# A two-layer graph network on one core: transposes a step ahead, node stages in three places of a step

## The chip, the cores and the metric

The kernel runs on one core of a Trainium2 chip. The metric is the device time in microseconds of one launch; the number given for a kernel is the median of several launches. Besides, one launch is recorded by the hardware profiler, and everything said of single instructions comes from that recorded launch.

## The reference

A graph of N = 6250 nodes with 256 features, and E = 106250 directed edges (50000 in both directions and a loop at each node), sorted by destination. All is fp32. With x the nodes and `e` the edge features, the reference computes, for layer 0,

```
msg = relu(x[src] + e);            agg = segment_sum(msg, dst)
h   = x + x + agg;                 f   = gelu(bn1(h) @ W1.T + b1) @ W2.T + b2
x1  = layernorm(x + bn2(h + f))
```

and for layer 1, on x1,

```
m    = gelu((x1[src] + e) @ W1m + b1m) @ W2m + b2m
mean = segment_sum(m, dst) / max(degree, 1)
u    = gelu(mean @ W1u + b1u) @ W2u + b2u
out  = layernorm(x1 + layernorm(x1 + u) * gamma + beta)
```

## The kernel before, in words

**Tiles, windows, blocks.** The edges are cut into 831 tiles of 128, and eight tiles make a window (SPAN), in two groups of four: 104 windows. Nodes are taken in 25 blocks of 256 (24 full ones and a rest of 106). Because edges are sorted by destination, the edges of a window end in a short run of nodes, in one block or in two neighbours; a block is complete after some 4.2 windows.

**What a window goes through.** `gather` (L768, L772) fetches the source rows of its eight tiles, with one indirect DMA per tile on GpSimd's queue (POOL), into one of five ring buffers. `lifted` (L804) copies a pair of edge tiles into a PSUM bank on ScalarE (ACT), and `add_to_gathered` (L812) adds that on VectorE (DVE) to the gathered rows in place. `activated` (L820) applies ReLU or GELU to a group of four tiles on ACT. `one_hots` (L828) makes eight 128x32 one-hot matrices on DVE. `into_slots` (L847) multiplies them with the eight tiles on TensorE (PE), which sums the edges of each of up to 128 slots, and ACT copies the sums out of PSUM. `into_blocks` (L863) multiplies the sums with a second one-hot matrix and so adds them to the block's accumulator, in layer 0 also the degrees (L886 on PE, L890 on DVE). In layer 0, `opened_0` (L1000) starts an accumulator with eight products of the block's own rows (L1006).

**Products with W1m.** Both layers need products of edge rows with W1m. Layer 1 takes x1 @ W1m + b1m, which the node stages of layer 0 have stored as `proj`, gathers its rows by source, and adds e @ W1m. `turned` (L779) transposes a pair of edge tiles on PE (four transposes, L785) into the one bank of `eaP`, and ACT copies them to SBUF (`eaT`, L790, three buffers). `product` (L793) multiplies them with W1m on PE (L798). Layer 0 computes those products for the first group of each window and stores them (`z`, L1032 and L1040, then `zst`); layer 1 loads these and computes the products for the second group.

**Node stages.** When a block is complete, a generator computes its rows: `nodes_0` (L919) has four yields, `nodes_1` (L1082) has four as well. In layer 0 the first stage copies and scales the accumulator (ACT L924, DVE L929); the second is PE L935 and GELU on ACT L940; the third is PE L948 and L953, then on DVE two adds (L958, L959) and `normalized` (L893, with a square root on ACT, L900, and two scalings L905) and the store of x1; the fourth transposes x1 on PE (L970) and copies on ACT (L973); the last is PE L979, DVE L983 and the store of proj. In layer 1: a mean (L1086 to L1090), twice PE L1100 with DVE L1105 and GELU L1109, then ACT L1115, DVE L1119, PE L1125, DVE L1129 to L1136 with one normalisation, and then the second normalisation and the store.

**Order.** `manual_schedule` (L737) means that every engine executes its instructions in the order in which the program issues them. A pass over a layer is a loop of steps; `step_0(v)` (L1015) loads edges for window v + 3 (SyncE's queue), gathers and makes the products for window v, adds and activates window u = v - 1, and sums window w = v - 2. `step_1` (L1165) has its products in window u. `advance` (L912) is called once at the end of a step and moves every running generator by one stage; a block that has been completed in the step is begun after that.

In a step of layer 0, PE executes: transposes of the first pair, slot sums of w, transposes of the second pair, product of the first, block sums of w, product of the second, then node stages. ACT's order: eaT of the first pair, two lifts, sums, eaT of the second, ReLU of the first group, two lifts, ReLU of the second group, nodes. DVE's order: the second one-hot matrix, two adds, copy of z, two adds, one-hots, degrees, copy of z, nodes. In layer 1, the GELU of the second group stands at the end, before the nodes.

**PSUM.** Eight banks: two for accumulators, one for slots, one for transposes (`eaP`), four (`workP`) taken in turn by lifts, products, degrees and node stages.

Of the kernel before, what the change touches and what calls it, by code (L numbers as in the profile page):

```python
# [14 lines left out]
P = 128  # L15
# [487 lines left out]
def kernel(  # L503
# [224 lines left out]
    with (  # L728
# [7 lines left out]
        tc.tile_pool(name="workP", bufs=4, space=bass.MemoryType.PSUM) as psw,  # L736
# [9 lines left out]
        def work():  # L746
            return psw.tile([P, 2, D], F32, name="workP")

# [163 lines left out]
        def advance():  # L912

            for gen in list(running):
                if next(gen, "done") == "done":
                    running.remove(gen)


        def nodes_0(b, acc, xb, deg):  # L919
# [11 lines left out]
            ps = work()  # L931
            gT = npool.tile([P, KC, SB], F32, name="gT")
            for o in range(KC):
                for k in range(KC):
                    nc.tensor.matmul(  # L935
                        ps[:, o, :width], lhsT=w1t_sb[:, k, o * P : (o + 1) * P],
                        rhs=fT[:, k, :width], start=(k == 0), stop=(k == KC - 1),
                    )
            for o in range(KC):
                nc.scalar.activation(  # L940
                    gT[:, o, :width], ps[:, o, :width], AF.Gelu, bias=col["L0_gnn_b1"][:, o : o + 1]
                )
            yield
            ps = work()
# [12 lines left out]
            ps = ps[:n, :H, :]  # L957
            nc.vector.tensor_add(ps, ps, xb[:n, :H, :])  # L958
            nc.vector.tensor_add(ps, ps, bn2_b[:n, None, :].to_broadcast([n, H, D]))  # L959
            x1 = npool.tile([P, SH, D], F32, name="x1")  # L960
            normalized(x1, ps, n, H)
# [4 lines left out]
            x1T = npool.tile([P, KC, SB], F32, name="x1T")  # L966
            ps = work()
            for h in range(H):
                for k in range(KC):
                    nc.tensor.transpose(  # L970
                        ps[:, k, h * P : h * P + n], x1[:n, h, k * P : (k + 1) * P], ident[:n, :n]
                    )
            nc.scalar.copy(x1T[:, :, :width], ps[:, :, :width])  # L973
            yield
            y = npool.tile([P, SH, D], F32, name="y")
            ps = work()
            for h in range(H):
                for k in range(KC):
# [3 lines left out]
                    )  # L982
            nc.vector.tensor_add(  # L983
# [30 lines left out]

        def step_0(v):  # L1015
            u, w = v - 1, v - 2
            if v + AHEAD < V:
                load_0(v + AHEAD)
            if v < V:
                gather(v, x)  # L1020
                first = turned(v, 0, 0, eas[v, 0])
                z = ep.tile([P, G, D], F32, name="z", bufs=2)
            if 0 <= w:
                slot_nodes(w)
            if 0 <= u < V:
                for q in (0, 2):
                    add_to_gathered(u, 0, q, lifted(u, 0, q, eas[u, 0]))
            if 0 <= w:
                into_slots(w, D + 1)
            if v < V:  # L1030
                second = turned(v, 0, 2, eas[v, 0])
                nc.vector.tensor_copy(z[:, 0:2, :], product(*first))  # L1032
            if 0 <= u < V:
                activated(u, 0, AF.Relu)
                for q in range(0, len(tiles_of(u, 1)), 2):
                    add_to_gathered(u, 1, q, lifted(u, 1, q, eas[u, 1]))
                one_hots(u)
            full = into_blocks(w, acc, opened_0, degs) if 0 <= w else []
            if v < V:
                nc.vector.tensor_copy(z[:, 2:4, :], product(*second))  # L1040
                nc.sync.dma_start(out=zst[v], in_=z.rearrange("p j d -> p (j d)"))
            if 0 <= u < V:
                activated(u, 1, AF.Relu)
            advance()
            for b in full:
                gen = nodes_0(b, acc.pop(b), xbs.pop(b), degs.pop(b))
                next(gen)
                running.append(gen)
# [33 lines left out]
        def nodes_1(b, acc, x1, deg):  # L1082
# [11 lines left out]
            yield  # L1094
            uT = npool.tile([P, UC, SB], F32, name="uT")
            for i in range(0, UC, 2):
                ps = work()
                for o in (i, i + 1):
                    for k in range(KC):
# [3 lines left out]
                        )  # L1103
                for o in (i, i + 1):
# [8 lines left out]
                yield  # L1113
# [8 lines left out]
            ps = work()  # L1122
            for h in range(H):
                for k in range(UC):
# [3 lines left out]
                    )  # L1128
            nc.vector.tensor_add(ps[:n, :H, :], ps[:n, :H, :], r[:n, :H, :])  # L1129
# [10 lines left out]
            yield  # L1140
            normalized(y, ps, n, H)
# [23 lines left out]
        def step_1(v):  # L1165
            u, w = v - 1, v - 2
            if v + AHEAD < V:
                load_1(v + AHEAD)
            if v < V:
                gather(v, proj)  # L1170
            if 0 <= w:
                slot_nodes(w)
            some = 0 <= u < V
            if some:
                first = turned(u, 1, 0, eas[u, 1])
                for q in (0, 2):
                    add_to_gathered(u, 0, q, lifted(u, 0, q, eas[u, 0]))
            if 0 <= w:
                into_slots(w, D)
            if some:  # L1180
                second = turned(u, 1, 2, eas[u, 1])
                add_to_gathered(u, 1, 0, product(*first))
                activated(u, 0, AF.Gelu)
                one_hots(u)
            full = into_blocks(w, acc_1, opened_1) if 0 <= w else []
            if some:
                add_to_gathered(u, 1, 2, product(*second))
                activated(u, 1, AF.Gelu)
            advance()
            for b in full:  # L1190
                gen = nodes_1(b, acc_1.pop(b), x1s.pop(b), degs_1.pop(b))
                next(gen)
                running.append(gen)

        for v in range(AHEAD):
            load_0(v)
        for v in range(V):
# [73 lines left out]
```

## Time and profile before

| | |
|---|---|
| time, median of three launches | 2784.48 us (2783.35 to 2786.59) |
| the profiled launch, its own time | 2831.86 us |
| its span in the profile | 2830.0 us |
| mean granted TensorE clock | 0.889 |
| layer 0, 60 to 1357 us of the span | PE busy 1053.98, DVE 689.88, ACT 680.85, POOL 767.36 |
| between the layers, 1357 to 1480 us | PE busy 54.14, POOL 57.35 |
| layer 1, 1480 to 2785 us | PE busy 982.15, DVE 666.55, ACT 614.76, POOL 730.11 |

How to read it. PE is TensorE's matmuls, PEld its weight loads, which run beside them. Every fp32 matmul leaves two records in this trace, so a product of a pair, four instructions, leaves eight[...]. The end of a matmul is worked out from its size and not observed. A line of a group or of a timeline gives the start, the time, the engine and the source line, then output and inputs by their names, and in brackets how long the engine had been idle before and who ended that wait. Who released a wait is inferred: of several signals it is the one that came last by the profile. "remote" is a release by something that the profile does not show. The profiled launch is 47.4 us slower than the median launch, so a sum over its durations is made against 2831.86 us and then scaled.

### The profile page before, as it was taken

The numbers are of one execution on the slowest core, as the hardware profiler recorded it, in microseconds if no ns is written. First come the engines' busy times: TensorE is split into PE (matmuls) and PEld (weight loads), VectorE is DVE, ScalarE is ACT, GpSimd is POOL, SyncE is SP. The second block draws the span as 40 slices with busy tenths as digits, with TensorE's granted clock in tenths as the row PEclk, the third lists the DMA queues.
The fourth block names the chain that finished last, engine by engine and source line by source line (L and its number), as shares of the span: only waits on it lengthen the run. The fifth ranks groups of instructions, "written<-read, shape, count | busy, mean of one in ns | idle before, by whom it ended". The sixth has DMA issues, their size and how long they took to land.

```text
span 2830.0 us, 38426 instructions
## 1 busy us (share of the span) xinstructions
PE 2125.9 (75%) x11916; PEld 1607.0 (57%) x11916; DVE 1430.2 (51%) x4130; ACT 1348.9 (48%) x2143; POOL 1575.0 (56%) x1671
## 2 busy tenths in 40 slices
PE   2588888888888888888637777777777777777776
PEld 1465656665665666656425555655555556565554
DVE  3355555555555555556314554455455555454455
ACT  1355555555555555556313444454444444454454
POOL 4666566566566566564266555555556565565550
PEclk8799899899899999899868888988998898898988
DMA  6577677677777777675445555545555554555440
GB/s 197 177 233 222 224 229 224 221 230 227 224 226 220 231 230 232 220 226 177 152 129 178 165 171 181 164 159 182 172 165 183 166 181 156 168 185 169 160 152 11
DMA packets 313740, 531.79 MB, mean 188 GB/s; under 512 B 37989, under 2 KB 233144, under 8 KB 313400
## 3 DMA queue, kind: packets, MB, share of 16 engines
q1 hardware_dynamic: 231190, 307.82, 32.4%
q0 software_dynamic: 79744, 217.71, 26.1%
q10 hardware_dynamic: 2594, 3.71, 0.4%
q8 instruction: 100, 1.64, 0.2%
q14 instruction: 112, 0.92, 0.1%
HBM read 455.34 MB, written 73.75 MB: 187 GB/s over the span
## 4 chain that ended last, share of the span: by engine, by line
PE 50%; issue 18%; DVE 10%; POOL 7%; ACT 6%; another core or an unknown queue 5%; DMA 3%; POOLq 0%; DVEq 0%; SPq 0%; ACTq 0%
PE workP L798 22%; PE slotP L855 8%; POOL ring L772 7%; PE eaP L785 6%; PE acc L879 4%; DVE ring L816 2%; ACT eaT L790 2%; ACT ring L824 1%; PE workP L1125 1%; PE workP L1100 1%; PE workP L979 1%; DMA ring<-proj,src_sb 1%; PE workP L935 1%; PE workP L886 1%
## 5 line engine op out<-in xcount | busy, mean ns | idle before, releaser
L772 POOL DMA_INDIRECT ring<-proj,src_sb x831 | 787.5, 948 | 640.7 <-PE slotP L855 322.8
L772 POOL DMA_INDIRECT ring<-in_x_dram,src_sb x831 | 785.7, 945 | 531.8 <-PE slotP L855 239.0
L798 PE MATMUL workP<-w1m_sb,eaT 128*128 128x256 f32 x3324 | 944.6, 435 | 10.3 <-issue 6.6
L816 DVE TENSOR_TENSOR ring<-workP,ring 128x512 f32<-128x512 f32 x832 | 541.0, 683 | 668.9 <-PE workP L798 148.8
L824 ACT ACTIVATE ring<-ring 128x1024 f32<-128x1024 f32 x418 | 439.5, 1052 | 833.2 <-DVE ring L816 627.6
L798 PEld LDWEIGHTS workP<-w1m_sb,eaT 128*128 128x128 f32 x3324 | 707.5, 223 | 137.0 <-issue 24.8
L855 PE MATMUL slotP<-ring,hot 128*32 128x257 f32 (+1 forms) x3324 | 376.2, 409 | 270.4 <-ACT ring L824 164.1
L785 PE MATMUL eaP<-ident,ea 128*128 128x128 f32 x1662 | 299.1, 309 | 258.8 <-ACT eaT L790 184.6
L785 PEld LDWEIGHTS eaP<-ident,ea 128*128 128x128 f32 x1662 | 213.5, 155 | 386.7 <-ACT eaT L790 261.4
L855 PEld LDWEIGHTS slotP<-ring,hot 128*32 128x32 f32 x3324 | 139.6, 111 | 428.9 <-ACT ring L824 202.3
L790 ACT COPY eaT<-eaP 128x512 f32<-128x512 f32 x416 | 242.1, 582 | 228.4 <-PE slotP L855 119.3
L809 ACT COPY workP<-ea 128x512 f32<-128x512 f32 x624 | 344.9, 589 | 0.0
L879 PE MATMUL acc<-hot,sums 128*128 128x160 f32 (+19 forms) x1360 | 237.0, 303 | 101.5 <-DVE hot L873 62.1
L879 PEld LDWEIGHTS acc<-hot,sums 128*128 128x128 f32 x1360 | 216.5, 205 | 134.2 <-issue 92.1
L833 DVE TENSOR_SCALAR hot<-ramp,slot 128x32 f32<-128x32 f32 x1662 | 268.4, 256 | 0.0
L890 DVE TENSOR_TENSOR degs<-degs,workP 1x160 f32<-1x160 f32 (+24 forms) x170 | 40.3, 243 | 226.3 <-PE slotP L855 97.9
L1032 DVE COPY z<-workP 128x512 f32<-128x512 f32 x104 | 71.7, 689 | 153.6 <-PE workP L798 71.2
L1040 DVE COPY z<-workP 128x512 f32<-128x512 f32 x104 | 71.1, 684 | 148.7 <-PE slotP L855 90.9
L900 ACT ACTIVATE mv<-mv,eps 128x2 f32<-128x2 f32 (+1 forms) x75 | 22.2, 295 | 192.1 <-DVE mv L899 180.0
L1100 PE MATMUL workP<-fT,w 128*128 128x256 f32 (+1 forms) x400 | 94.7, 381 | 0.5 <-DVE fT L1090 0.5
L900 ACT ACT_TABLE_LOAD x73 | 93.7, 1283 | 1.3
L1125 PE MATMUL workP<-w2u_sb,uT 128*128 128x256 f32 (+1 forms) x392 | 89.0, 379 | 3.4 <-ACT uT L1109 3.4
(109 smaller groups left out, 1460.2 us busy)
## 6 DMA issues: line engine op xcount, KB each, us to landing
ea<-in_edge_attr_dram SPq DMA_DIRECT2D x310, 512.0 KB
zst<-z SPq DMA_DIRECT2D x104, 512.0 KB
ea<-zst SPq DMA_DIRECT2D x104, 512.0 KB
ring<-in_x_dram,src_sb POOLq DMA_INDIRECT x831
ring<-proj,src_sb POOLq DMA_INDIRECT x831
xb<-in_x_dram SPq DMA_DIRECT2D x24, 256.0 KB
x1d<-x SPq DMA_DIRECT2D x24, 256.0 KB
proj<-y SPq DMA_DIRECT2D x24, 256.0 KB
```

The lines of the kernel that those rows point to most:

```text
L772: nc.gpsimd.indirect_dma_start(out=rings[v % RING][:n, g * G + j, :D], out_offset=None, in_=table, in_offset=bass.IndirectOffsetOnAxis(ap= ...
L785: nc.tensor.transpose(pe[:, j, k, :n], ea[:n, q + j, k * P : (k + 1) * P], ident[:n, :n])
L790: nc.scalar.copy(eaT[:, j:k, :, :n], pe[:, j:k, :, :n])
L798: nc.tensor.matmul(ph[:n, j, :], lhsT=eaT[:, j, k, :n], rhs=w1m_sb[:, k, :], start=(k == 0), stop=(k == KC - 1),)
L809: nc.scalar.copy(ps[:n, j:k, :], of[:n, q + j : q + k, :])
L816: nc.vector.tensor_add(r[:n, at + j : at + k, :D], ps[:n, j:k, :], r[:n, at + j : at + k, :D])
L824: nc.scalar.activation(at, at, func)
L833: nc.vector.tensor_scalar(hots[v][:n, j, :], ramp[:n, :SLOTS], slot[:n, t : t + 1], None, op0=ALU.is_equal,)
L855: nc.tensor.matmul(ps[q * SLOTS : (q + 1) * SLOTS, :width], lhsT=hot[:n, j, :], rhs=r[:n, j, :width], start=(i == 0), stop=(i == PAIR - 1 ...
L879: nc.tensor.matmul(acc[b][:, k, cols], lhsT=its[:, k * P : (k + 1) * P], rhs=at, start=(begins and k == 0), stop=(last_span[b] == v and k ...
L1100: nc.tensor.matmul(ps[:, o - i, :width], lhsT=w12[:, k, o * P : (o + 1) * P], rhs=mT[:, k, :width], start=(k == 0), stop=(k == KC - 1),)
L1125: nc.tensor.matmul(ps[:n, h, :], lhsT=uT[:, k, h * P : h * P + n], rhs=w2u_sb[:, k, :], start=(k == 0), stop=(k == UC - 1),)
```

## The change

The instructions of every engine and the DMAs are the same in number. What differs is their order, their PSUM banks and how the node stages are cut.

- **Banks.** `workP` has three banks instead of four; a new pool `nodeP` has one, and the PE stages of the nodes take theirs from it.
- **Node stages.** `advance` moves only the oldest running generator, by one stage, and is called three times a step: before the product of the first pair, after the block sums, and at the end of the step. The generators yield more often: what PE does in a stage and what ACT or DVE do with its result are now two stages. A completed block is begun (`begin`) directly after the block sums, ahead of the second call of `advance`.
- **Transposes.** `turned` is issued one step before its `product`: in layer 0 for window v + 1 in step v, in layer 1 for window v in step v while products are those of v - 1. Both pairs of the first window are transposed before the first step. The first pair's transposes stand behind the first product, the second pair's behind the second product.
- **Places in the step.** In layer 0 the ReLU of the second group and the one-hots come ahead of the second product, and the degrees on DVE ahead of the second group's adds. In layer 1 the GELU of the second group comes behind the transposes for the next step and their copy on ACT, and the one-hots after the block sums.

The core of the diff (node stages of layer 0 cut to their yields, those of layer 1 left out but for the last part):

```diff
-        tc.tile_pool(name="workP", bufs=4, space=bass.MemoryType.PSUM) as psw,
+        tc.tile_pool(name="workP", bufs=3, space=bass.MemoryType.PSUM) as psw,
+        tc.tile_pool(name="nodeP", bufs=1, space=bass.MemoryType.PSUM) as psn,
...
         def advance():
-            for gen in list(running):
-                if next(gen, "done") == "done":
-                    running.remove(gen)
+            while running and next(running[0], "done") == "done":
+                running.pop(0)
...
         def nodes_0(b, acc, xb, deg):
...
             yield
-            ps = work()
-            gT = npool.tile([P, KC, SB], F32, name="gT")
+            ps = node_work()
             for o in range(KC):
                 for k in range(KC):
                     nc.tensor.matmul(
...
                     )
+            yield
+            gT = npool.tile([P, KC, SB], F32, name="gT")
             for o in range(KC):
                 nc.scalar.activation(
...
             yield
-            ps = work()
+            ps = node_work()
             for h in range(H):
...
+            yield
-            ps = ps[:n, :H, :]
-            nc.vector.tensor_add(ps, ps, xb[:n, :H, :])
+            of = ps[:n, :H, :]
+            nc.vector.tensor_add(of, of, xb[:n, :H, :])
...
         def step_0(v):
-            u, w = v - 1, v - 2
-            if v + AHEAD < V:
-                load_0(v + AHEAD)
-            if v < V:
+            u, w, t = v - 1, v - 2, v + 1
+            adds, slots, mults, turns = 0 <= u < V, 0 <= w < V, 0 <= v < V, t < V
+            if mults:
+                if v + AHEAD < V:
+                    load_0(v + AHEAD)
                 gather(v, x)
-                first = turned(v, 0, 0, eas[v, 0])
                 z = ep.tile([P, G, D], F32, name="z", bufs=2)
...
             if adds:
                 for q in (0, 2):
                     add_to_gathered(u, 0, q, lifted(u, 0, q, eas[u, 0]))
             if slots:
                 into_slots(w, D + 1)
-            if v < V:
-                second = turned(v, 0, 2, eas[v, 0])
-                nc.vector.tensor_copy(z[:, 0:2, :], product(*first))
             if adds:
                 activated(u, 0, AF.Relu)
+            advance()
+            if mults:
+                nc.vector.tensor_copy(z[:, 0:2, :], product(*eaTs.pop((v, 0))))
+            if turns:
+                eaTs[t, 0] = turned(t, 0, 0, eas[t, 0])
+            if slots:
+                begin(into_blocks(w, acc, opened_0, degs), nodes_0, acc, xbs, degs)
+            advance()
+            if adds:
                 for q in range(0, len(tiles_of(u, 1)), 2):
                     add_to_gathered(u, 1, q, lifted(u, 1, q, eas[u, 1]))
+                activated(u, 1, AF.Relu)
                 one_hots(u)
-            full = into_blocks(w, acc, opened_0, degs) if 0 <= w else []
-            if v < V:
-                nc.vector.tensor_copy(z[:, 2:4, :], product(*second))
+            if mults:
+                nc.vector.tensor_copy(z[:, 2:4, :], product(*eaTs.pop((v, 2))))
                 nc.sync.dma_start(out=zst[v], in_=z.rearrange("p j d -> p (j d)"))
-            if 0 <= u < V:
-                activated(u, 1, AF.Relu)
+            if turns:
+                eaTs[t, 2] = turned(t, 0, 2, eas[t, 0])
             advance()
...
         def step_1(v):
...
             if adds:
                 activated(u, 0, AF.Gelu)
+            advance()
+            if adds:
+                add_to_gathered(u, 1, 0, product(*eaTs.pop((u, 0))))
+            if turns:
+                eaTs[v, 0] = turned(v, 1, 0, eas[v, 1])
+            if slots:
+                begin(into_blocks(w, acc_1, opened_1), nodes_1, acc_1, x1s, degs_1)
+            advance()
+            if adds:
                 one_hots(u)
+                add_to_gathered(u, 1, 2, product(*eaTs.pop((u, 2))))
+            if turns:
+                eaTs[v, 2] = turned(v, 1, 2, eas[v, 1])
+            if adds:
                 activated(u, 1, AF.Gelu)
             advance()
```

In `nodes_1` the two halves of L1100 are two stages on PE, each followed by a stage with DVE L1105 and ACT L1109; the adds of L1119 join the second of those; the two halves of L1125 are two stages; then one stage for DVE L1129 to L1136, and one for the second normalisation and the store. So in layer 0 a block that begins in step s does PE L935 in its second place and GELU in its third; in step s + 1 PE L948/L953, DVE's adds and normalisation, and PE L970; in step s + 2 ACT L973, PE L979 and DVE L983.

## The prediction

> **What bounds the kernel now.** I read the busy shares first, then the table of waits, then timelines of single steps, and last the distance between the gathers of successive steps, counted from the gathers' own start times.
>
> ```profile
> PE 2125.9 (75%) x11916; PEld 1607.0 (57%) x11916; DVE 1430.2 (51%) x4130; ACT 1348.9 (48%) x2143; POOL 1575.0 (56%) x1671
> ```
>
> No engine is full. POOL's 56% understates it: a gather is 0.945 us of work and 0.30 us of issue, 1.25 us each, eight to a step. That is 10.0 us a step, 208 steps, 2080 us of a span of 2830.0.
>
> ```profile
> ACT ring L824 <- DVE ring L816: 627.6, 191, 29.3
> POOL ring L772 <- PE slotP L855: 561.8, 231, 11.5
> PEld eaP L785 <- ACT eaT L790: 261.4, 144, 28.1
> DVE ring L816 <- remote: 126.2, 21, 44.6
> ```
>
> Columns: total us, times, longest. POOL waits 561.8 us for the slot matmuls, 231 times: about once a step, 2.4 us each. Yet nobody is busy then, which a timeline shows:
>
> ```profile
> 799.45 0.38 PE L855 MATMUL slotP<-ring,hot 128*32 128x257 f32 x1 [1.04 <-issue]
> 800.18 0.40 PE L855 MATMUL slotP<-ring,hot 128*32 128x257 f32 x1 [0.35 <-issue]
> 800.90 0.38 PE L855 MATMUL slotP<-ring,hot 128*32 128x257 f32 x1 [0.32 <-issue]
> 800.97 0.30 DVE L890 TENSOR_TENSOR degs<-degs,workP 1x156 f32<-1x156 f32 x1 [2.06 <-PE slotP L855]
> 801.18 0.58 ACT L790 COPY eaT<-eaP 128x512 f32<-128x512 f32 x1 [3.53 <-PE slotP L855]
> 801.21 0.67 DVE L1040 COPY z<-workP 128x512 f32<-128x512 f32 x1
> 801.40 0.94 POOL L772 DMA_INDIRECT ring<-in_x_dram,src_sb  x1 [2.28 <-PE slotP L855]
> ```
>
> ACT's copy of a transpose and DVE's copy of a product both start near 801.2 although PE did those transposes and products before the slot matmuls (transposes at 795.89, products ending 796.05): the news of them came about 5 us late, and then all consumers went at once, 2 us after POOL's last gather (798.18 + 0.95). The same at a larger size where POOL issues 35 gathers in a row:
>
> ```profile
> 1409.07 0.95 POOL L772 DMA_INDIRECT ring<-proj,src_sb  x1 [0.30 <-issue]
> ...
> 1450.32 0.95 POOL L772 DMA_INDIRECT ring<-proj,src_sb  x1 [0.30 <-issue]
> 1453.51 0.69 DVE L816 TENSOR_TENSOR ring<-workP,ring 128x512 f32<-128x512 f32 x1 [44.59 <-remote]
> 1455.74 0.50 PEld L879 LDWEIGHTS acc<-hot,sums 128*128 128x128 f32 x2 [45.08 <-issue]
> ```
>
> DVE and PE stand still until the run of gathers has landed. So I read a loop: the slot matmuls' signal frees a ring slot, POOL issues eight gathers (10.0), they land (2.0), PE's signals held meanwhile come through, the next slot signal frees POOL. That is 12.0 us a step. Last gather to last gather measures 12.0 at the median of layer 0 (mean 12.44) and 12.0 in the quarter of layer 1's steps that are quickest (mean 13.25). I counted what passes in layer 0: of PE's completions in the first 3 us of such a run 321 of 359 are seen at once; between 4 and 7 us 81 of 215; the largest count by far, 693, is seen in the twelfth microsecond, where 102 end.
>
> [...]
>
> **The change part by part.** Counts of PE, ACT, DVE and POOL instructions and all DMAs stay; only order, banks and the size of node stages change. SP's loads keep their place at the head of a step, and the node stores (x1d, proj, out) come one to two steps earlier on SP; nothing on SP waits long, so I price that at zero, and at most one 0.5 us issue a block if it delays a load three steps ahead.
>
> (1) *Transposes one step ahead.* Takes the wait PEld L785 <- ACT (261.4 us) and its PE half off the head of products. But that wait lies inside the 12.0 us loop, where PE is ahead of POOL anyway. In a layer 0 step without nodes: flush, z copy 0.69, product 1.92, transposes 0.6, blocks 1.2, product 1.92, transposes 0.6 all end by 8 us; the slot matmuls of the next step then run at 8 to 9 us and are held to 12. Gain 0, loss 0 (were the cover gone, transposes and copy would cost 1.2 a step, 125 us). In layer 1 the last GELU now stands behind the eaT copy (0.58) but that runs beside the add (0.68): 0, at most +1.0 a step if the two transposes are held where the product is not.
>
> (2) *Three work banks.* The next lift or product waits for the z copy at L1040, 0.69 us after the flush; covered by the 10 us of gathers: 0. Without that cover it is 0.69 a step, 72 us in layer 0.
>
> (3) *Node stages of layer 0.* This is where I see the cost. Begin step: PE L935 after the blocks, its GELUs at the step's end, on ACT behind the eaT copy, which waits for transposes done some 10 us into the gathers, so for the flush. After it: copy 0.58, table 1.28, two GELUs 0.93, so 2.8 us. Next step: PE's L948/L953 are issued ahead of the first product, wait for these GELUs and take 2.6 us: they end 5.4 us into the new gathers. By the counts above some four in ten of such signals pass, some of them left over from earlier; I take 0.65 as held. When held, everything DVE has to do for it comes after the flush: z copy 0.69, degs 0.24, two adds 1.37 (L958, L959), statistics 1.19 (two of 0.414 and 0.182), table 1.28 and square root 0.30, reciprocal 0.17, two scalings 1.08, and then PE's four transposes 0.45, which stand on PE *ahead of the next slot matmuls*: 6.8 us in which POOL has nothing to do. Before, those transposes and the slots were a step apart, and the whole node work cost layer 0 only 0.44 us a step, 46 us over 104 steps (12.44 less 12.0), which is 1.8 a block. So: 25 blocks x 0.65 x 6.8 = 110, less 46 = +64. The next step meets degs ahead of the adds and an opening block (L1006, 1.16) under a full DVE: 0 to 2.2 us a block, I take 1.1: +27.
>
> (4) *Node stages of layer 1.* Node work costs 1.25 us a step now (13.25 less 12.0), 130 us. After: L1100 i=0 behind the blocks, its second half and L1125's second half ahead of the first product (1.75 each), norm ahead of the last product's add and GELU. I add the chains of the three node steps and of the plain one to 13.2, 13.0, 14.3 and 12 to 13: 13.3 on the mean, so 0, from -65 (half of what nodes cost goes) to +104 (1.0 a step, the upper bound of part 1).
>
> (5) *The turn between layers* (1357 to 1480 us, PE at 54.14 busy of 123.00): node generators end in fewer steps; -10, from -15 to +5.
>
> Sum: 64 + 27 + 0 - 10 = +81 on the profiled execution of 2831.86 us. That stands 47.4 above the median of the runs, 1.7%; scaled by 0.983 it is +80, so 2784.5 + 80 = 2865 us. Its own range, from the bounds of the held share (0.4 to 1.0: -43 to +60), the next step (-27 to +28), is 2800 to 2950.
>
> **The rivals.** *A, faster.* PE2's signal passes and both layers sink to the 12.0 loop. For: two of three in the middle of a run are held, not all, and shorter stages give PE gaps to fill. Against: GELU's start at the flush. Layer 0 -46, layer 1 -50, turn -10: -106, x 0.983, 2680 us. It decides when the L948/L953 matmuls end within 3 us of the start of POOL's run.
>
> *B, no change.* POOL's loop hides both orders: layer 0 keeps its 46 us, layer 1 its 130: 2784 us. For: POOL is the loop in most steps. Against: the new PE order puts a DVE-fed transpose before the slots.
>
> *C, slower in both layers.* In layer 1 the last GELU follows a held eaT copy: +1.0 x 104 = 104 on top of 81: 185, x 0.983, 2966 us. For: ACT executes in order, and the transposes' signal falls at 5 to 6 us of the run. Against: the product's own signal does as well, and was waited for before.
>
> That the edit doesn't do what it says is excluded only for counts; a lost overlap is what I forecast.
>
> **How the numbers follow.** Forecast 0.50, A 0.28, B 0.06, C 0.16. Some 0.02 of the forecast's chance ends below 2779 and 0.01 within 0.2%: faster 0.30, within 0.2% (about what a measurement of this kernel can tell from no change) 0.06, slower 0.64. Half of A (0.14) lies below 2680 and somewhat over a third of C (0.06) above 2980: the range is 2680 to 2980.
>
> **What would show it.** Right: gathers 17 to 19 us apart once a block in layer 0, POOL there waiting for PE L855, PE's x1 transposes waiting for DVE; 12.0 in the other steps. Wrong: a mean of 12.0 to 12.3 in layer 0, or the L958 add starting within 1 us of L953's end. For A: layer 1 below 12.8; for C: above 13.8 with ACT's eaT copy ahead of the last GELU.

## The result and the profile after

The change made the kernel slower: 3094.92 us (3087.37 to 3103.14) against 2785.53 us (2783.35 to 2799.45) for the kernel before, a ratio of 1.110 (1.105 to 1.115). I had forecast 2865 us and a range up to 2980. The direction was right, the size by far too small: +309 us where I had +80.

The profiled launch took 3103.14 us, its span is 3101.2 us. PE's busy time rose by 88 us with the same instructions, and that of no other engine by more than 1.5%. Page of the kernel after, busy time:

```profile
PE 2214.2 (71%) x11916; PEld 1647.1 (53%) x11916; DVE 1437.1 (46%) x4130; ACT 1368.2 (44%) x2143; POOL 1574.5 (51%) x1671
```

Where the time went, by stage. The table counts from ACT's copies of the slot sums, one per window: their first to their last in a layer, and between the layers. A second profiled launch of the kernel before stands beside the first, because the first took some 47 us longer than the median and the second did not. PE was busy 2063.7 us in the second, so against that its busy time rose by 150 us.

| us | layer 0 | between | layer 1 |
|---|---|---|---|
| before, first profile | 1266 | 62 | 1373 |
| before, second profile | 1246 | 57 | 1339 |
| after | 1478 | 82 | 1415 |
| after less the second | +232 | +25 | +76 |

Seven tenths are layer 0. Of its 97 steps in full run, by the distance of POOL's last gathers, 23 take 18.83 us on the mean, one for nearly each block; 19 more lie between 13.5 and 18.3; the other 55 average 12.2. Above 12.2 us the 23 are worth 153 us and the 19 are worth 76.

POOL's wait moved to another releaser, and PE now waits for the nodes. The kernel after, table of waits (total us, times, longest):

```profile
POOL ring L776 <- ACT eaT L794: 577.1, 154, 13.5
...
PE nodeP L956 <- ACT gT L947: 100.2, 25, 5.7
...
PE nodeP L979 <- DVE x L909: 31.2, 19, 5.2
```

The same matmuls in the two kernels, groups by line (busy, mean ns of one, then PE's idle time just before them). First before, where they are L948, L970 and, in layer 1, L1100:

```profile
L948 PE MATMUL workP<-w2s_sb,gT 128*128 128x256 f32 (+1 forms) x196 | 51.4, 385 | 0.0
L970 PE MATMUL workP<-ident,x 128*128 128x128 f32 (+1 forms) x98 | 15.3, 277 | 4.1 <-DVE x L905 4.1
L1100 PE MATMUL workP<-fT,w 128*128 128x256 f32 (+1 forms) x400 | 94.7, 381 | 0.5 <-DVE fT L1090 0.5
```

And after:

```profile
L956 PE MATMUL nodeP<-w2s_sb,gT 128*128 128x256 f32 (+1 forms) x196 | 84.4, 577 | 100.2 <-ACT gT L947 100.2
L979 PE MATMUL nodeP<-ident,x 128*128 128x128 f32 (+1 forms) x98 | 17.5, 305 | 31.2 <-DVE x L909 31.2
L1127 PE MATMUL nodeP<-fT,w 128*128 128x256 f32 (+1 forms) x400 | 102.9, 403 | 62.8 <-DVE fT L1116 25.4
```

PE waited 0.0 us for the GELUs of a block before and waits 100.2 now, 25 times, once a block; and the mean record of a matmul takes 577 ns there instead of 385: directly after the wait they are slower, as the timeline below shows (four records in 2.07 us, and the four of the second half in 1.11). With L939 (0.0 before, 9.7 after), PE's idle time ahead of these four groups rose from 4.6 to 203.9 us.

One such step of layer 0, a timeline of the kernel after (start, duration, then the idle time before and its releaser in brackets):

```profile
592.41 0.60 PE L789 MATMUL eaP<-ident,ea 128*128 128x128 f32 x4
...
596.61 0.58 ACT L794 COPY eaT<-eaP 128x512 f32<-128x512 f32 x1 [4.16 <-PE slotP L859]
597.21 1.28 ACT L947 ACT_TABLE_LOAD   x1
597.32 0.94 POOL L776 DMA_INDIRECT ring<-in_x_dram,src_sb  x1 [2.48 <-ACT eaT L794]
598.50 0.84 ACT L947 ACTIVATE gT<-nodeP,cols_sb 128x256 f32<-128x256 f32 x2
...
599.39 2.07 PE L956 MATMUL nodeP<-w2s_sb,gT 128*128 128x256 f32 x4 [4.03 <-ACT gT L947]
...
602.11 1.11 PE L956 MATMUL nodeP<-w2s_sb,gT 128*128 128x256 f32 x4
...
605.71 0.69 DVE L1058 COPY z<-workP 128x512 f32<-128x512 f32 x1 [4.56 <-PE workP L802]
...
606.32 0.43 PE L890 MATMUL workP<-hot,sums 128*1 128x161 f32 x2
...
608.60 0.31 DVE L894 TENSOR_TENSOR degs<-degs,workP 1x161 f32<-1x161 f32 x1 [2.19 <-remote]
608.84 0.68 DVE L968 TENSOR_TENSOR nodeP<-nodeP,xb 128x512 f32<-128x512 f32 x1
...
612.03 0.99 DVE L909 TENSOR_SCALAR x<-nodeP,mv 128x256 f32<-128x256 f32 x2
613.09 0.66 PE L979 MATMUL nodeP<-ident,x 128*128 128x128 f32 x4
614.15 1.25 DVE L837 TENSOR_SCALAR hot<-ramp,slot 128x32 f32<-128x32 f32 x8
614.43 2.07 PE L859 MATMUL slotP<-ring,hot 128*32 128x257 f32 x16 [0.69 <-DVE hot L837]
615.82 0.94 POOL L776 DMA_INDIRECT ring<-in_x_dram,src_sb  x1 [8.80 <-ACT eaT L794]
```

Read it as one chain. ACT's GELU comes behind the eaT copy (its table load and itself); PE's L956 waits 4.03 us for it, and behind L956 on PE waits the first product; behind that product's copy to z on DVE waits the normalisation, although its own input was ready; behind the normalisation wait the x1 transposes on PE and the one-hots on DVE; behind both wait the slot sums; and POOL has stood for 8.80 us when it may gather again. Which engine waits for which follows from the fixed orders. Two links are longer than the orders alone make them, because news from PE comes late: the eaT copy starts 3.6 us after its transposes ended (593.01 us), and the addition of the degrees, which stands ahead of the normalisation, 1.85 us after L890 ended (606.75 us). In the first 22 blocks these two delays have medians of 2.9 and 1.4 us. The z copy, on the other hand, starts 0.04 us after its product in the median block.

### The profile page after: what moved, and what is told of

Read it like the earlier page. It is cut to its first block, busy times and chain, and to the rows that moved or that the text cites. A ratio compares the mean times of both kernels' runs of the same rounds, so it can differ in the third digit from the quotient of the medians.

```text
span 3101.2 us, 38495 instructions
## 1 busy us (share of the span) xinstructions
PE 2214.2 (71%) x11916; PEld 1647.1 (53%) x11916; DVE 1437.1 (46%) x4130; ACT 1368.2 (44%) x2143; POOL 1574.5 (51%) x1671
## 5 line engine op out<-in xcount | busy, mean ns | idle before, releaser
L802 PE MATMUL workP<-w1m_sb,eaT 128*128 128x256 f32 x3324 | 942.7, 433 | 246.2 <-DVE degs L894 94.2
L802 PEld LDWEIGHTS workP<-w1m_sb,eaT 128*128 128x128 f32 x3324 | 697.0, 218 | 454.8 <-DVE degs L894 108.9
L859 PE MATMUL slotP<-ring,hot 128*32 128x257 f32 (+1 forms) x3324 | 392.7, 453 | 304.9 <-ACT ring L828 246.5
L859 PEld LDWEIGHTS slotP<-ring,hot 128*32 128x32 f32 x3324 | 154.3, 119 | 455.6 <-ACT ring L828 307.6
L789 PE MATMUL eaP<-ident,ea 128*128 128x128 f32 x1662 | 270.7, 289 | 12.3 <-ACT eaT L794 12.3
L789 PEld LDWEIGHTS eaP<-ident,ea 128*128 128x128 f32 x1662 | 227.0, 152 | 66.7 <-ACT eaT L794 15.4
L883 PEld LDWEIGHTS acc<-hot,sums 128*128 128x128 f32 x1360 | 191.8, 198 | 85.0 <-issue 63.3
L1058 DVE COPY z<-workP 128x512 f32<-128x512 f32 x104 | 71.8, 691 | 206.2 <-PE workP L802 142.0
L956 PE MATMUL nodeP<-w2s_sb,gT 128*128 128x256 f32 (+1 forms) x196 | 84.4, 577 | 100.2 <-ACT gT L947 100.2
L1127 PE MATMUL nodeP<-fT,w 128*128 128x256 f32 (+1 forms) x400 | 102.9, 403 | 62.8 <-DVE fT L1116 25.4
L865 ACT COPY sums<-slotP 128x257 f32<-128x257 f32 (+1 forms) x208 | 77.6, 373 | 104.8 <-PE slotP L859 50.8
L1159 PE MATMUL nodeP<-w2u_sb,uT 128*128 128x256 f32 (+1 forms) x392 | 120.5, 462 | 2.0 <-DVE uT L1134 2.0
```

The source lines that it names most:

```text
L789: nc.tensor.transpose(pe[:, j, k, :n], ea[:n, q + j, k * P : (k + 1) * P], ident[:n, :n])
L802: nc.tensor.matmul(ph[:n, j, :], lhsT=eaT[:, j, k, :n], rhs=w1m_sb[:, k, :], start=(k == 0), stop=(k == KC - 1),)
L859: nc.tensor.matmul(ps[q * SLOTS : (q + 1) * SLOTS, :width], lhsT=hot[:n, j, :], rhs=r[:n, j, :width], start=(i == 0), stop=(i == PAIR - 1 ...
L883: nc.tensor.matmul(acc[b][:, k, cols], lhsT=its[:, k * P : (k + 1) * P], rhs=at, start=(begins and k == 0), stop=(last_span[b] == v and k ...
L1127: nc.tensor.matmul(ps[:, o - i, :width], lhsT=w12[:, k, o * P : (o + 1) * P], rhs=mT[:, k, :width], start=(k == 0), stop=(k == KC - 1),)
L1159: nc.tensor.matmul(ps[:n, h, :], lhsT=uT[:, k, h * P : h * P + n], rhs=w2u_sb[:, k, :], start=(k == 0), stop=(k == UC - 1),)
```

## The experiments

Runs were spread over several chips, and each has its own run of the kernel before on the same chip beside it, so ratios are compared and not times. On all chips but one the kernel before took 2775 to 2787 us; on the chip of the runs with one edit of the changed kernel each (x1 turns late, adds first, both, last GELU first) it took 2215 us. In the two runs without gathers, plain loads of consecutive rows stand in for the gathers, and the indexing by source is left out.

| run | time, us | before on that chip | ratio (95%) |
|---|---|---|---|
| before, no gathers | 2182.2 | 2786.8 | 0.781 (0.777 to 0.785) |
| after, no gathers | 2520.2 | 2786.8 | 0.902 (0.898 to 0.906) |
| turns only | 2801.3 | 2786.8 | 1.005 (1.003 to 1.007) |
| nodes only | 2993.7 | 2786.8 | 1.071 (1.066 to 1.076) |
| x1 turns late | 2472.2 | 2215.1 | 1.116 (1.114 to 1.118) |
| adds first | 2615.1 | 2215.1 | 1.180 (1.178 to 1.182) |
| both | 2579.3 | 2215.1 | 1.164 (1.162 to 1.166) |
| last GELU first | 2444.6 | 2215.1 | 1.102 (1.099 to 1.106) |
| after again | 3101.3 | 2775.4 | 1.114 (1.109 to 1.120) |
| spaced | 2828.7 | 2775.4 | 1.017 (1.013 to 1.021) |
| before again | 2779.4 | 2783.3 | 1.000 (0.998 to 1.001) |
| layer 1 turns | 2771.3 | 2783.3 | 0.996 (0.994 to 0.997) |
| layer 1 turns, GELU first | 2758.5 | 2783.3 | 0.991 (0.989 to 0.993) |

**Does the loss need signals that are held behind gathers?** That was my theory: PE's news arrives late while POOL gathers, so that the node work comes after it. The rival: the orders of the engines alone.

```diff
-                    nc.gpsimd.indirect_dma_start(
-                        out=rings[v % RING][:n, g * G + j, :D],
-                        out_offset=None,
-                        in_=table,
-                        in_offset=bass.IndirectOffsetOnAxis(ap=src_sb[:n, t : t + 1], axis=0),
-                    )
+                    r0 = t * P % (table.shape[0] - P)
+                    nc.sync.dma_start(
+                        out=rings[v % RING][:n, g * G + j, :D], in_=table[r0 : r0 + n, :]
+                    )
```

> The kernel before, with each of POOL's 1662 indirect gathers replaced by a plain load of as many consecutive rows on SyncE's queue; it leaves out the indexing by source, all else is as before. Held-signal theory (PE's completion signals reach ACT and DVE late while POOL runs gathers): the 12.0 us loop is gone and steps are bound by PE's own work, about 2126 us busy plus waits: 2350 us (2250 to 2500). Order theory (each engine's fixed order alone sets the step): the loop stays, 2700 to 2800 us.

> The changed kernel, with the same replacement of the gathers by plain loads of consecutive rows; it leaves out the indexing by source. Held-signal theory: the loss of the change goes with the gathers; 60 us under to 40 us over the same edit of the kernel before. Order theory (the chain GELU, L956, normalisation, transposes, slots costs 6 us a block whatever POOL does): still 200 us or more over the same edit of the kernel before.

Without gathers the kernel before takes 2182.2 us, even less than I expected: the gathers do set its 12.0 us loop, which I had read rightly. But the changed kernel takes 2520.2, 338 us or 15% more. A loss as large is there without one gather, and my theory that it goes with the gathers falls. It is not the same loss, however. By the same stage table, layer 0 takes 1011 us before and 1187 after, layer 1 1036 and 1205: +175 and +168, where with gathers it was +232 and +76. So part of layer 0's loss does go with the gathers, and layer 1 loses more without their cover. The plain loads may have a share as well: DVE's wait for them in layer 0 is 91.8 us before and 142.0 after, which no run separates. A timeline of the changed kernel without gathers shows the same chain in layer 0, with waits of under 2 us at each link (its lines are numbered two lower):

```profile
514.48 0.84 ACT L945 ACTIVATE gT<-nodeP,cols_sb 128x256 f32<-128x256 f32 x2
...
515.38 1.13 PE L954 MATMUL nodeP<-w2s_sb,gT 128*128 128x256 f32 x4 [1.87 <-ACT gT L945]
...
521.61 0.68 DVE L966 TENSOR_TENSOR nodeP<-nodeP,xb 128x512 f32<-128x512 f32 x1
...
524.80 1.00 DVE L907 TENSOR_SCALAR x<-nodeP,mv 128x256 f32<-128x256 f32 x2
...
525.85 0.66 PE L977 MATMUL nodeP<-ident,x 128*128 128x128 f32 x4 [1.69 <-DVE x L907]
526.91 1.25 DVE L835 TENSOR_SCALAR hot<-ramp,slot 128x32 f32<-128x32 f32 x8
527.20 2.94 PE L857 MATMUL slotP<-ring,hot 128*32 128x257 f32 x16 [0.69 <-DVE hot L835]
```

**Which half of the change?** One run has the transposes ahead and the new order inside the step, with the node stages, banks and `advance` of before; the other has the node stages, three places and banks, with transposes and order of before. The first cut is written against the changed kernel, the second against the kernel before.

```diff
 turns only
-            advance()
...
-            begin(into_blocks(w, acc, opened_0, degs), nodes_0, acc, xbs, degs)
+            full[:] = into_blocks(w, acc, opened_0, degs)
...
             advance()
+            begin(full, nodes_0, acc, xbs, degs)
 nodes only
+            advance()
             if v < V:
                 second = turned(v, 0, 2, eas[v, 0])
...
-            full = into_blocks(w, acc, opened_0, degs) if 0 <= w else []
+            if 0 <= w:
+                begin(into_blocks(w, acc, opened_0, degs), nodes_0, acc, xbs, degs)
+            advance()
```

> Only the transposes a step ahead and the new order inside the step; node stages cut as before, all of them at the end of the step, in four shared banks. Held-signal theory: layer 0 keeps its 12.0 us loop, apart from degrees ahead of the second group's adds where a window opens a block (+30 us); layer 1 pays 0.8 us a step for its last GELU behind the copy of held transposes (+85): about 2900 us (2840 to 2930). If the node places carry the whole loss: 2785 us.

> Only the node stages in three places a step with their own bank (and three work banks); transposes and everything else in the order of the kernel before. Held-signal theory: PE still has the x1 transposes ahead of the next slot sums, and DVE's normalisation comes after the signals are let through, 5 to 6.5 us a block in layer 0 (+125 to +160), layer 1 somewhat better (-30): about 2905 us (2860 to 2960). If the transposes carry the loss: 2785 us or less.

Transposes ahead cost 0.5% (I had 4%); the node places alone 7.1%, above my range. Halves of +14 and +207 make 221 of the 309 to 326 us: some 90 to 105 come only when both are there. The stage table says where: layer 0 spans 1278 us with turns only, 1320 with nodes only, 1478 with both. In the order of before, DVE makes a window's second adds and one-hots ahead of the block sums, so they are not behind a normalisation; in the new order they are. That this is the reason is not shown; the run with the adds first below, on another chip, lost by undoing it. Layer 1 is the reverse: 1470 with nodes only, 1319 with turns only, 1415 with both.

**Which link holds the slot sums?** Two edits of the changed kernel's layer 0, and both together, and one of its layer 1.

```diff
 x1 turns late
             nc.sync.dma_start(out=rows_of(x1d, b), in_=x1[:n, :H, :])
             yield
+            yield
 adds first
+            if adds:
+                for q in range(0, len(tiles_of(u, 1)), 2):
+                    add_to_gathered(u, 1, q, lifted(u, 1, q, eas[u, 1]))
+                activated(u, 1, AF.Relu)
+                one_hots(u)
             if slots:
                 begin(into_blocks(w, acc, opened_0, degs), nodes_0, acc, xbs, degs)
             advance()
-            if adds:
-                for q in range(0, len(tiles_of(u, 1)), 2):
-                    add_to_gathered(u, 1, q, lifted(u, 1, q, eas[u, 1]))
-                activated(u, 1, AF.Relu)
-                one_hots(u)
 last GELU first
+            if adds:
+                activated(u, 1, AF.Gelu)
             if turns:
                 eaTs[v, 2] = turned(v, 1, 2, eas[v, 1])
-            if adds:
-                activated(u, 1, AF.Gelu)
```

> The changed kernel with one empty place between a block's normalisation in layer 0 and the transposes of x1, so that these stand behind the next slot sums on PE instead of ahead. Theory now (the orders on DVE and PE together): alone it brings little, since the one-hots that the slot sums need are queued behind the normalisation on DVE as well: 3085 us (3060 to 3100). Rival (the place of the x1 transposes on PE is the whole loss of layer 0): 5 us a block and more, 2960 us or less.

> The changed kernel with the second group's adds, ReLU and one-hots ahead of the block sums, degrees and the second place, in layer 0. Theory now: degrees no longer delay the adds in windows that open a block (-45), while in the step of the normalisation the slot sums still stand behind the x1 transposes: 3050 us (3010 to 3085). Rival (normalisation ahead of the adds on DVE is the whole loss): 2900 us or less.

> Both edits together. Theory now: only now are the slot sums free of the normalisation, and a block costs some 2 us instead of 6.3: -110 on top of the -45, 2935 us (2890 to 2985), far more than the two edits' own gains together. Rival (each edit acts alone, or something else holds the slots): no more than the sum of the two.

> The changed kernel with layer 1's GELU of the second group ahead of the transposes for the next step and their copy on ACT. If plain steps of layer 1 went from 12.0 to 12.9 us by waiting for that copy: -0.8 us a step, 3015 us (2990 to 3050). If layer 1 lost to its node places instead: 3095 us, within 10.

The chip was the one on which the kernel before takes 2215 us, and the changed kernel itself was not run there, so the expected times can't be held against these. What can: the last run leaves layer 0 as changed, and the other three leave layer 1 as changed. Layer 1 spans 1220, 1220 and 1215 us in those and 1219 in the last, so the last GELU's place was worth nothing there, and 2444.6 us stands for the changed kernel. So the change costs 10% on this chip too, where PE's signals are not late (see the last section too): in the first 22 blocks the eaT copy starts 0.09 us after its transposes in the median, not 2.9, and the degrees 0.04 us after L890.

But the loss lies elsewhere. POOL in the run with the last GELU first:

```profile
L776 POOL DMA_INDIRECT ring<-in_x_dram,src_sb x831 | 786.6, 947 | 309.8 <-issue 136.8
L776 POOL DMA_INDIRECT ring<-proj,src_sb x831 | 786.4, 946 | 470.9 <-issue 256.8
```

A gather takes 0.946 us and the next is issued 0.30 us later, so 831 back to back take an estimated 1037 us. On this chip the gathers of layer 0 take 1063 us from the first's start to the last's end, those of layer 1 1182; on the other chips the changed kernel's take 1489 and 1407, the second profile of the kernel before 1264 and 1318. The kernel before was not profiled here, but it cannot gather faster than back to back: of the 230 us at most 26 are the gathers of layer 0 and at most 145 those of layer 1, the rest lies around them. POOL stands for 8.85 us behind this chain in the median block of the changed kernel above (of the same 22), and in the median block here it does not wait at all: the chain is there, but the gathers cover it. So the order alone is enough for a loss, but the large loss in layer 0, with gathers, stands only where signals are late.

The three edits of layer 0 could therefore gain at most 26 us on this chip, and cannot tell which link holds the slot sums on the others. What they can show is a cost. Against 2444.6, the late x1 transposes cost 28 us. The reason that I gave for "alone it brings little" shows in the waits: the wait of PE for x1 (46.9 us) is gone, but PE's waits ahead of the slot sums rose from 184.7 to 251.8 us, the one-hots' share of it from 54.0 to 112.3. Moving the adds first, from which I expected a gain, cost 171 us, and both edits 135. The groups of the run with adds first show where half of it is:

```profile
L939 PE MATMUL nodeP<-fT,w1t_sb 128*128 128x256 f32 (+1 forms) x200 | 83.4, 591 | 42.0 <-ACT fT L928 41.2
L979 PE MATMUL nodeP<-ident,x 128*128 128x128 f32 (+1 forms) x98 | 26.1, 419 | 92.9 <-DVE x L909 92.9
```

The adds, lifts and ReLU now stand between the block sums and fT on ACT, and ahead of the normalisation on DVE, but the PE stages that wait for these stayed where they were: L939 waits 42.0 us instead of next to none, L979 92.9 instead of 46.9. This suggests that not one link counts but the distance between a PE stage and what it waits for. That is the theory I went on with.

**The test of the distance.** The changed kernel, with PE's part of a node stage only at the end of a step, and its ACT or DVE part only ahead of the first product of the next. Transposes, banks and the rest of the order stay as changed, but in layer 1 the two halves of one product (L1159, L1125 before) become one stage.

```diff
-        def advance():
-            while running and next(running[0], "done") == "done":
-                running.pop(0)
+        due = {}
+        def advance(place=None):
+            while running and place in (None, due[running[0]]):
+                gen = running[0]
+                due[gen] = next(gen, "done")
+                if due[gen] != "done":
+                    break
+                running.pop(0)
...
                 activated(u, 0, AF.Relu)
-            advance()
+            advance("rest")
...
-            advance()
             if adds:
                 for q in range(0, len(tiles_of(u, 1)), 2):
...
                 eaTs[t, 2] = turned(t, 0, 2, eas[t, 0])
-            advance()
+            advance("PE")
```

> The changed kernel as it is, as the base for what runs beside it. Where PE's signals are held behind the gathers, 3095 us beside 2785 for the kernel before; where the kernel before takes some 2215 us because they are not, 2460 us (2430 to 2560), so slower by 10 to 15% either way, if the loss is one of order; if the loss needs held signals, within 2% of the kernel before in the second case.

> The changed kernel with one PE stage of the nodes a step, at the end of the step, and the ACT or DVE part of it ahead of the first product of the next step, so that a PE stage stands a third of a step or more behind what it waits for; transposes, banks and order otherwise as changed. Theory now (a PE stage stands directly behind the ACT or DVE work that it waits for, and the slot sums wait behind it on PE): nearly the whole loss goes, to within 2% of the kernel before on the same chip. Rival (transposes ahead, three work banks and degrees ahead of the adds carry a good part of the loss): still 4% or more above it.

From 1.114 to 1.017: of 326 us lost on that chip, 273 are gone, though transposes ahead, three work banks and degrees ahead of the adds are all still there. Layer 0 spans 1271 us, in place of 1475 in the run beside it, with 3 steps above 18.3 us and 4 from 13.5 to 18.3. PE's idle time ahead of the four groups fell to 22.9 us; of these, the two shown above:

```profile
L962 PE MATMUL nodeP<-w2s_sb,gT 128*128 128x256 f32 (+1 forms) x196 | 52.0, 389 | 1.9 <-ACT gT L953 1.9
L985 PE MATMUL nodeP<-ident,x 128*128 128x128 f32 (+1 forms) x98 | 20.1, 342 | 7.3 <-DVE x L909 7.3
```

That shows the cutting and placing of the node stages to be the cause of most of the loss. It does not separate distance from number: a block has one PE stage a step here, and up to two in the changed kernel (L956 and L979 stand in one step). Nor was it run on the chip of 2215 us. Of the 53 us that remain, the stage table puts 25 in layer 0 and 30 between the layers, against the second profile of the kernel before.

**What is left, and a version that beats both.** The kernel before again, and the kernel before with only layer 1's transposes a step ahead and its new order, without node places; then the same with the last GELU first.

```diff
 layer 1 turns: step_0, nodes, banks and advance as before; in step_1
-                first = turned(u, 1, 0, eas[u, 1])
...
-                second = turned(u, 1, 2, eas[u, 1])
-                add_to_gathered(u, 1, 0, product(*first))
+                add_to_gathered(u, 1, 0, product(*eaTs.pop((u, 0))))
+            if turns:
+                eaTs[v, 0] = turned(v, 1, 0, eas[v, 1])
...
+                add_to_gathered(u, 1, 2, product(*eaTs.pop((u, 2))))
+            if turns:
+                eaTs[v, 2] = turned(v, 1, 2, eas[v, 1])
+            if adds:
                 activated(u, 1, AF.Gelu)
```

> The kernel before as it is, for a second profile: its first profiled launch took 47 us more than its median. If that is the cost of being profiled, again 45 us or so above; if it was that one launch, within 15 us of its median, with layer 1 some 30 us shorter in the profile. Either way a median within 0.5% of the base.

> The kernel before in layer 0 and in its node stages and banks; in layer 1 alone the transposes a step ahead with the changed order inside the step. The run with transposes ahead in both layers had layer 1 at 12.66 us a step against 13.14, so if that gain is layer 1's own: -30 to -50 us, 1 to 2% under the kernel before. If it was only a different profiled launch: no change, within 0.3%.

> The same with layer 1's last GELU ahead of the transposes for the next step and their copy on ACT. If the GELU waits for the copy in plain steps: another -0.5 us a step, 50 us under the previous kernel. If the product's own signal comes no earlier than the transposes': the same as the previous kernel, within 0.5%.

The second profile of the kernel before has a span of 2771.6 us, so the first was an odd launch: layer 1 is 34 us shorter in the second, layer 0 20 us. Layer 1 turns gains 12 us, between my two expectations: layer 1 spans 1315 us against 1339, and 14 of these 24 are given back between the layers (71 against 57). With the last GELU first it is 2758.5 us, 0.9% under the kernel before on that chip, the lowest ratio of all kernels here with the whole computation; the GELU's place is worth 13 us, not 50.

## Why the prediction was wrong, point by point

**The bound.** Right, on the chips that it was read from: the kernel is held to a loop of gathers of 12.0 us, and taking the gathers out brought it to 0.781. Right too that plain steps of layer 0 would stay: 55 of 97 average 12.2 us. "Nothing on SP waits long", though, was misread: in the profile before, the loads of layer 1 at L1158 wait 763.8 us on SyncE's queue in 62 waits, up to 33.3; whether their order cost anything was not tried.

**(1) Transposes ahead.** Priced at 0 in layer 0, and 0 to +1.0 us a step in layer 1. Alone they measure +14 us in all: by the stage table +32 in layer 0, +13 between the layers and -21 in layer 1. There they gain again in the kernel with layer 1's transposes only, 24 us, so the sign of that bound was wrong; the last GELU behind the eaT copy was worth 13 us, 0.13 a step.

**(2) Three work banks.** Priced at 0. PE waited 94.2 us for degrees ahead of products, in the table of waits after; but the spaced run keeps 82.5 us of it and most of the time comes back, so it is largely covered. The three banks, and the one bank for the nodes, were not run alone.

**(3) Node stages of layer 0: this is the step that failed, by its size.** Forecast +64 and +27, measured +232 (+212 against the first profile, from which the sum was made). I had the steps (17 to 19 us once a block; 18.8 measured), the GELU's start behind a late eaT copy, and the chain's end (x1 transposes ahead of the slot sums). The 1.28 us that I counted for a table load is what the profile before shows: 1283 ns for each of the 73 at L900 and of the 25 ahead of the GELUs at L940. What was wrong is "I take 0.65 as held", the condition that I put on the rest of the chain. It hits 23 of 97 steps, nearly every block. The reason stands in the timeline: whether L956's signal is late at 604 us does not matter to DVE, because the z copy stands ahead of the normalisation and its product stands on PE behind L956. L956 and L961 together took 4.3 us in that step, not 2.6. Over the first 22 blocks their median is 4.8 us behind a wait with a median of 4.2, and 2.9 us behind waits of 1.9 on the chip of 2215 us. So the term is 23 steps x 6.6 us = 153, not 110. The credit of 46 did not come either: plain steps went to 12.2 us, not 12.0, against a mean of 12.44 in the first profile before and 12.24 in the second, which leaves 25 and 4 us. The second term failed by more: "0 to 2.2 us a block, I take 1.1: +27" measured 19 steps with 76 us together. I priced there what a wait for degrees and an opening block add, and not that the next step has a PE stage (L991) and starts from queues that are already late. Which share is whose was not separated; the degrees' order alone is not it, since spacing keeps it and has only 7 such steps in all.

**(4) Node stages of layer 1.** A second term that failed: priced at 0, measured +76 us against the second profile (+42 against the first). The steps average 13.76 us from gather to gather, against the 13.3 that I added up. Nodes only makes it 1470, spacing makes it 1343: here too it is the node places, with PE waiting 62.8 us for the mean (L1116, L1114) ahead of L1127, a few us after the block sums. I had laid those chains end to end without asking how long each PE stage would wait.

**(5) The turn.** -10 forecast, +20 to +25 measured. On the chips with late signals every kernel with either half of the change has a longer turn: 71 to 87 us with transposes ahead, 83 with the nodes only, against 57 to 62. Why was not tried.

**My rivals.** None had it: all three took the held signals as given, and differed in what these would hide. The one that was missing is that the order costs as much in all on a chip or in a program without them, though in other places: on the chip at most 26 us of the 230 lie in the gathers of layer 0, and the program loses alike in both layers (175 and 168 us). The base was worth 47 us as well: the profile that I measured layer 1's step from (13.25 us) was an odd launch, and the second gives 12.85.

## What to carry to other kernels

When a chain that runs over three engines is cut into finer stages, count for each stage what it waits for and how much other work stands between the two on *its own* engine: before, PE's L948 stood a whole step behind its input and waited 0.0 us for it; a third of a step was too little with up to two PE stages of a block in a step (the same stage waited 100.2 us), and enough where a PE stage had one place a step to itself (1.9 us). Ask next what is queued behind the wait: in the step shown above, PE's 4.03 us at L956 were paid by the product, then by the slot sums, then by the gathers, which stood for 8.80 us. And a theory that explains the bound need not explain the loss: take the bound out of both kernels and look whether the difference stays, and in which stage. Here the sum stayed while the places changed, and the sum alone had hidden that.

## What the runs showed of the hardware that I had not expected

The same kernel before took 2775 to 2787 us on several chips and 2215 us on another. On that one the signals are not late: the eaT copies of the blocks start 0.09 us after their transposes in the median (2.9 on another chip), and POOL's wait for slot sums is small although it gathers as much. Waits of the changed kernel with the last GELU first, on that chip:

```profile
POOL ring L776 <- PE slotP L859: 74.6, 131, 1.9
```

There ACT copies the first slot sums at 53 us of the span, in the middle of the opening run of gathers, and not at 92 us after it, and the gathers take the same 946 ns. In the changed kernel without gathers, on a chip where the kernel before takes 2786.8 us, the two eaT copies of the step at 510 to 521 us start 0.10 and 0.09 us after their transposes. Why PE's signals come late on the other chips while POOL gathers is not shown by any run here. The change costs 10 to 11% on both kinds: where signals are late, 232 us of it in layer 0 and 76 in layer 1; where they are not, at most 26 us in the gathers of layer 0 and at most 145 in those of layer 1, of 230.
